# A four-layer graph network on one core: where masks are made, when they are counted, and how resident and loaded blocks are mixed

## The chip, the core and the metric

The kernel runs on one core of a Trainium2 chip. The metric is the device time of one execution in microseconds (us). The kernel before was run three times: 551.85, 552.71 and 555.07 us, median 552.71 us.

The engines are named as the profile names them: PE (matrix multiply, with PEld for its weight loads), DVE (vector), ACT (scalar), POOL (GpSimd) and SP, which here only issues transfers (DMAs). [...] A "q" after an engine's name in a profile line means its sequencer, which waits or issues and does not compute.

## The reference, cut to what matters

The input is a node matrix `x` (3327 x 64) and a dense weighted adjacency matrix `adj` (3327 x 3327). Four layers follow, each of the form `x = layernorm(x + layer(x, adj))`. The change touches the third and the fourth:

```python
# layer 2: two hops
for k in range(2):
    agg = adj @ x
    x = tanh(concatenate([agg, x], axis=1) @ W[k])
...
# layer 3: of each row's neighbours only the last 100 count, with weights halved step by step
support = input @ weight
mask = (adj != 0)
rank = cumsum(mask, axis=1)
deg = rank[:, -1:]
k = minimum(deg, 100)
pos = rank - (deg - k)
w = mask * where(pos > 0, 0.5 ** (k - pos), 0.0)
out = w @ support + bias
```

So layer 3 needs, for every entry of `adj`, whether it is nonzero (the mask), and how many nonzeros stand behind it in its row (a running count).

## The kernel before, in words

**Tiling.** The nodes are padded to 3328 and cut into 26 blocks of 128. The host hands over `adj` transposed, so one block of it is a 128 x 3328 tile of f32 (1664 KB): 128 neighbours on the partitions, all nodes along the free axis. A half of a block is 128 x 1664, and a chunk is 416 columns; there are four chunks in a half.

**Hop 1 and hop 2 of layer 2** (the loop `for k in range(2)`) go through the 26 blocks. For each block, `add` (the matmuls of L514) issues 8 pairs of matmuls of 416 columns, which add the block's share to the four accumulators. Seven blocks lie in SBUF for the whole layer (`kept`: 25, 24, 23, 22 and 20, 21, 19). The others come by DMA into four rotating buffers (`at_l`) and a fifth (`bt_l`), issued on SP (`block`, L216). Such a buffer is free again when the PE has added the block and the DVE has made its mask, so these two set when the next load is issued. Hop 2 takes 23 blocks in its loop (steps 0 to 22: five that hop 1 left in the buffers, then 0, 25, 1, 24, 2, 23, 3, 22, then 4 to 13), and blocks 20, 21 and 19 after it, in `chunk_end`.

**Masks and counts beside hop 2.** Layer 3 needs, before it starts, for each block and each node how many nonzeros stand in the blocks behind it. For that, each block gets a bf16 mask on the DVE and 8 small matmuls on the PE (`t_counts`, L451), which add the block's column counts to two accumulators `t`. There are two kinds of mask:

- scratch masks (`t_masks`, L444), used for the count alone. They are made half by half into the tile `tm`, which holds one block; hop 2 has seven of them (blocks 0 to 6). A new one must wait until the PE has counted the last one.
- resident masks (`both_masks`, L353), which stay for layer 3. They are written over f32 blocks that hop 2 has already added: one f32 block has room for two bf16 masks (`slots_of`). The table `place` says at which step which mask goes where. Nine are made: block 25 into the tile `over` at step 1, blocks 24 and 23 at step 6, 22 and 20 at step 8, 21 and 19 at step 12, and the last two of the loop at steps 21 and 22.

When all 26 blocks are counted, `t_out` (L461) moves `t` to SBUF as `tb`, POOL writes it to DRAM as `t_rows` (L463), and `rows_of` (L431) reads one row of it back into the first partition of each resident mask.

**Between hop 2 and the loop of layer 3** ("the prologue" below) the last three blocks are added chunk by chunk (`chunk_end`), ACT takes tanh, the DVE adds the layer's input (`with_x2`, L725), and the layer norm and the node products of layer 3 follow in four groups of blocks A, B, C, E: `finish` (PE), `squares` (ACT), `sums`, `roots`, `factor`, `x3_of`, `rest_of` (DVE).

**The loop of layer 3** has 52 steps, 26 for each half. Step q: `count` (L644) multiplies mask q with a triangular matrix into one of two PSUM banks c = 0, 1; `read` turns the count into a weight by taking the bits of an integer (ACT at L659, or DVE at L657); `products` (L861) multiplies the weight with `support`, three steps later. Every seventh step the PE also does the low part of the products (L878). A count of the next step must wait until its bank is read. Bank 0 is always read by ACT, bank 1 by the DVE in odd steps and by ACT in even ones.

The masks of blocks that are not resident are loaded again by halves (`load`, L345, 832 KB each, four buffers `ah`), made on the DVE (`masks`, L366, six buffers), and get their first row from `t_rows` by a small DMA (L368). There are 34 of them, one at most in a step. SP issues in each such step the row and then the next load. The list `steps` puts seven of the nine resident blocks first in half 0, and spreads the other two among the 17 loaded ones.

A list `with_step` gives one small piece of remaining work to each of the first steps. At the fourth, `firsts_weighted` runs three DVE instructions (L478 to L480), which make the weights of the first rows from `tb` and a tile `m0`; `m0` holds one of the six mask buffers until then. At the seventh, `first_rows` (L893, L897) issues 16 small DMAs on POOL into `sf`, which the products four steps before the end of a half need (`first_products`, L904).

Order of the DVE's instructions in a step of the loop before, which the prediction uses:

```python
read(1, q, q % 2 == 1)          # DVE in odd steps
with_step.pop(0)()              # the step's piece of other work
masks(to_mask.pop(0))           # if a mask buffer is free
```

Of the kernel before, what the change touches and what calls it, by code (L numbers as in the profile page):

```python
# [81 lines left out]
def kernel(  # L82
# [230 lines left out]
    def layers(ctx, x2, x3, begun_here, kept, ready, ahead_ctx, strm):  # L313
# [168 lines left out]
        with tc.tile_pool(  # L482
# [6 lines left out]
            for k in range(2):  # L489
# [37 lines left out]
                if k:  # L527
                    end = [jb for jb in kept if jb not in soon]
                    r = len(order)
                    for jb in soon:  # L530
                        order += [others.pop(0), jb]
                    order += others
                    place = {
                        1: [(soon[0], over)],
                        r + 1: list(zip(soon[1:3], slots_of(soon[0]))),
                        r + 3: list(zip((soon[3], end[0]), slots_of(soon[1]))),
                        r + 7: list(zip(end[1:], slots_of(soon[3]))),
                    }
                    for i, at in zip((-2, -1), slots_of(soon[2])):
                        place[len(order) + i] = [(order[i], at)]  # L540
# [45 lines left out]
                for i, jb in enumerate(order):  # L586
# [6 lines left out]
                    if i or not k:  # L593
                        for c in range(CPH):
                            add(c, jb)
                    if k and len(t_made) > 2 * BATCH_T:
                        t_counts()
                    if jb not in t_done and jb not in kept and (k or i >= FIRST_T):
                        t_masks(jb)
                        if len(t_made) >= len(t_at):  # L600
                            t_counts()
                    if k:
                        for b, at in place.get(i, ()):
                            both_masks(b, at)
                    if k == 0 and begun_here:

                        if i == 8:
# [2 lines left out]

                            warm_t = small.tile([P, 1], F32, tag="warm", name="warm_t")
                            nc.scalar.activation(warm_t, hT[:, :1], AF.Tanh)
                    if k and len(t_done) == NB and not t_ends:
                        t_ends.append(i)
                        t_counts()
                        t_out()
                        rows_of(resident)
                if k:
# [266 lines left out]

        def first_rows():

            with nc.allow_non_contiguous_dma(reason="one row of each block"):
                for cg in range(CPH):
                    e = cg % 2  # L890
                    for h in range(2):
                        at = slice(cg * 32 + h * NBH, cg * 32 + (h + 1) * NBH)
# [129 lines left out]
        first_out = None  # L1022
        with_step = [
            lambda: other_parts(B), lambda: first_part(C), lambda: rest_of(C),
            lambda: (other_parts(C), firsts_weighted()), lambda: first_part(E), lambda: rest_of(E),
            lambda: (other_parts(E), first_rows()), lambda: x3_later(C), lambda: x3_later(E),
        ]
        products(0, 0)
        advance(1, 2)
        products(0, 1)  # L1030
        for q in range(LEAD, len(steps) + LEAD + 1):
            turn = q == NB + LEAD
            read(0, q, False)
# [5 lines left out]
            while consumed and consumed[0] <= q:  # L1039
                consumed.pop(0)  # L1040
# [1006 lines left out]
```

## Time and profile before

| what | value |
|---|---|
| median of three runs | 552.71 us |
| the profiled execution | 552.03 us |
| its span (first to last instruction) | 550.2 us |
| busy: PE, DVE, ACT, POOL | 93%, 71%, 53%, 42% of the span |
| hop 2, from its second step to its last (327.98 to 404.46 us) | 76.48 us, PE busy 71.86 |
| prologue (404.46 to 425.01 us) | 20.55 us, PE busy 18.24 |
| loop of layer 3, first stretch (425.01 to 479 us) | 53.99 us, PE busy 47.36 |
| loop, change of halves (479 to 500 us) | 21.00 us, PE busy 18.20 |
| loop, rest (500 to 537 us) | 37.00 us, PE busy 36.51 |

The span begins at the first instruction and ends at the last; the execution's own time is 1.8 us more. Times of day below are counted from the span's start. The stages were told apart by the lines of their instructions: hop 2 is where L514 reads `at_l`, `bt_l` and `kept` for the second time, the prologue begins with the first `chunk_end` that follows, and the loop with the first L861.

How to read the lines: in the timeline each line has the start, the length, the engine, the source line, the operation, what it writes and reads, the form, and how many instructions were merged; in brackets, how long the engine sat idle before it, and what released it. In the view of waits, each line names who waited, for whom, how long in total, how often, and the longest wait.

### The profile page before, as it was taken

The numbers are of one execution on the slowest core, as the hardware profiler recorded it, in microseconds if no ns is written. First come the engines' busy times: TensorE is split into PE (matmuls) and PEld (weight loads), VectorE is DVE, ScalarE is ACT, GpSimd is POOL, SyncE is SP. The second block draws the span as 40 slices with busy tenths as digits, with TensorE's granted clock in tenths as the row PEclk, the third lists the DMA queues.
The fourth block names the chain that finished last, engine by engine and source line by source line (L and its number), as shares of the span: only waits on it lengthen the run. The fifth ranks groups of instructions, "written<-read, shape, count | busy, mean of one in ns | idle before, by whom it ended". The sixth has DMA issues, their size and how long they took to land. (4 is left out here: it accounts for less than half of the span.)

```text
span 550.2 us, 7634 instructions
## 1 busy us (share of the span) xinstructions
PE 509.8 (93%) x2865; PEld 210.8 (38%) x2865; DVE 390.7 (71%) x563; ACT 293.3 (53%) x345; POOL 232.6 (42%) x121
## 2 busy tenths in 40 slices
PE   8889999999999999999999999888998789989992
PEld 5522222222222222854433354333444344454542
DVE  6899999999999999799444231637137986666314
ACT  4899999999999997610000000000016755566641
POOL 4599999999999998000000000000260280000000
PEclk9999999999999999899999999989999999999996
DMA  8978766666766545799998019957963799975001
GB/s 287 366 227 293 244 222 224 240 215 220 238 215 233 184 147 226 299 418 427 424 424 368 0 31 408 412 186 269 414 209 102 259 372 395 404 291 188 0 1 37
DMA packets 34137, 139.20 MB, mean 253 GB/s; under 512 B 11199, under 2 KB 12977, under 8 KB 28971
## 3 DMA queue, kind: packets, MB, share of 16 engines
q1 hardware_dynamic: 30571, 137.40, 67.3%
q0 software_dynamic: 1184, 0.63, 0.5%
q10 hardware_dynamic: 2336, 0.59, 0.5%
q8 instruction: 24, 0.39, 0.3%
q14 instruction: 22, 0.18, 0.1%
HBM read 136.93 MB, written 1.04 MB: 251 GB/s over the span
## 5 line engine op out<-in xcount | busy, mean ns | idle before, releaser
L1260 POOL TENSOR_TENSOR sg<-sg,at 128x1664 f32<-128x1664 f32 x44 | 163.6, 3738 | 1.3 <-ACT sg L1248 1.2
L1288 ACT ACTIVATE pq<-pq,al,ga 128x832 f32<-128x832 f32 x104 | 104.7, 1011 | 10.8 <-DVE a L1287 10.5
L1275 PE MATMUL pq<-riT,ljT 64*128 64x416 f32 x416 | 100.8, 561 | 10.4 <-DVE v L1296 6.2
L1296 DVE SCALAR_TENSOR_TENSOR v<-pq,a 128x832 f32<-128x832 f32 x104 | 105.8, 1018 | 3.2 <-ACT pq L1288 2.2
L1287 DVE SCALAR_TENSOR_TENSOR a<-pq,sg 128x832 f32<-128x832 f32 x104 | 105.7, 1016 | 0.5 <-PE prep_fours L1366 0.4
L1305 PE MATMUL acc<-v,xv 128*64 128x416 f32 x416 | 95.3, 537 | 0.0
L514 PE MATMUL cnt<-at_l,lj 128*64 128x416 f32 x496 | 90.1, 514 | 0.1
L1248 ACT ACTIVATE sg<-lb,rb 128x1664 f32<-128x1664 f32 (+1 forms) x53 | 87.2, 1649 | 0.0
L623 ACT ACTIVATE x<-cnt 128x416 f32<-128x416 f32 x8 | 4.1, 517 | 151.2 <-PE cnt L514 151.2
L659 ACT ACTIVATE w<-cnt 128x832 int16<-128x832 f32 x79 | 65.6, 864 | 34.9 <-PE cnt L644 34.4
L463 POOL DMA_DIRECT2D t_rows<-tb x4 | 2.6, 711 | 148.7 <-DVE tb L461 148.6
L1275 PEld LDWEIGHTS pq<-riT,ljT 64*128 64x128 f32 x416 | 31.3, 184 | 83.7 <-DVE v L1296 82.9
L514 PEld LDWEIGHTS cnt<-at_l,lj 128*64 128x64 f32 x496 | 34.9, 137 | 50.6 <-issue 49.3
L861 PE MATMUL acc<-w,s 128*128 128x416 bf16 x208 | 52.5, 339 | 1.3 <-DVE sq L765 0.5
L1305 PEld LDWEIGHTS acc<-v,xv 128*64 128x64 f32 x416 | 20.6, 134 | 61.8 <-issue 58.0
L657 DVE TENSOR_SCALAR w<-cnt 128x832 int16<-128x832 f32 x25 | 25.5, 1022 | 25.6 <-PE cnt L644 25.6
L514 PE MATMUL cnt<-kept,lj 128*64 128x416 f32 x224 | 43.4, 533 | 0.0
L366 DVE TENSOR_SCALAR mask<-ah 128x1664 bf16<-128x1664 f32 x34 | 35.5, 1058 | 7.0 <-DMA ah<-in_adjT 5.1
L644 PE MATMUL cnt<-mask,tri 128*128 128x416 bf16 x136 | 34.8, 338 | 6.0 <-DVE w L657 3.5
L444 DVE TENSOR_SCALAR tm<-at_l 128x1664 bf16<-128x1664 f32 x20 | 19.5, 1022 | 21.1 <-PE t L451 21.1
L644 PEld LDWEIGHTS <-tri 128*128 128x128 bf16 x208 | 19.5, 97 | 34.4 <-issue 17.7
L1260 POOL TENSOR_TENSOR sg<-sg,kept 128x1664 f32<-128x1664 f32 (+1 forms) x10 | 30.0, 3017 | 0.0
(316 smaller groups left out, 455.5 us busy)
## 6 DMA issues: line engine op xcount, KB each, us to landing
at_l<-in_adjT SPq DMA_DIRECT2D x27, 1664.0 KB, 11.7
at<-in_adjT SPq DMA_DIRECT2D x44, 832.0 KB, 4.8
ah<-in_adjT SPq DMA_DIRECT2D x34, 832.0 KB, 6.4
kept<-in_adjT SPq DMA_DIRECT2D x7, 1664.0 KB
bt_l<-in_adjT SPq DMA_DIRECT2D x6, 1664.0 KB
lb<-lf_rows SPq DMA_DIRECT2D x2, 384.0 KB, 5.7
mask<-t_rows SPq DMA_DIRECT2D x34, 3.2 KB
ljT<-ljT SPq DMA_DIRECT2D x4, 128.0 KB, 3.9
```

What stands on the lines that cost most here:

```text
L366: nc.vector.tensor_scalar(mask[q], ahead.pop(q), 0.0, None, ALU.not_equal)
L514: nc.tensor.matmul(acc[c][h * D : (h + 1) * D, :], hw[:, slot(jb), :], blocks[jb][:, o : o + CW], start=c not in begun, stop=last, skip_gr ...
L644: nc.tensor.matmul(cnt[c][:, e, :], tri, mask[q][:, of], start=True, stop=True, skip_group_check=True,)
L659: nc.scalar.activation(w.bitcast(I16), cnt[c], AF.Relu)
L861: nc.tensor.matmul(acc[h, c][:, e, :], s12[:, slot(jb)].rearrange("p t d -> p (t d)"), ws[q, c][:, e, :], start=first, stop=last,)
L1248: nc.scalar.activation(sg[:, :, of], lbs[:, :, of], AF.Sigmoid, bias=rb[:, sl : sl + 1])
L1260: nc.gpsimd.tensor_tensor(sg[:, :, of], sg[:, :, of], at[:, :, of], ALU.mult)
L1275: nc.tensor.matmul(pq[:, h, :], ljT[h != jb // NBH][rows, of], riT[rows, ch * CW : (ch + 1) * CW], start=True, stop=True,)
L1287: stt(a_s[t], pqs[t], CUBIC_PLUS, us.pop(t), op0=ALU.add, op1=ALU.mult)
L1288: nc.scalar.activation(pqs[t], pqs[t], AF.Square, bias=al[:, one], scale=ga[:, one])
L1296: stt(w, pqs.pop(t), CUBIC_REST, a_s.pop(t), op0=ALU.add, op1=ALU.mult)
L1305: nc.tensor.matmul(accs[cp, ci][h * D : (h + 1) * D, :], xv[:, slot(jb), :], w[:, h, :], start=(jb == orders[cp][0]), stop=(jb == orders[c ...
```

## The change

In hop 2:

- The table `place` has one resident mask in each of its steps instead of two: block 25 at step 1 as before, 24 at step 7, 22 at 9, 20 at 10, 21 at 13, 19 at 14, 23 at 17, and the last two as before.
- From step 6 on, scratch masks take turns between `tm` and the first half of block 25's space, which is free from then until block 23's mask goes there at step 17.
- `t_counts` is called in each step after the step's adds, and before the step's masks are made, so that a mask is counted in the step after the one in which it was made. The last one is counted at step 18, where it was step 15; `t_out` and the rows follow there.

Between hop 2 and the loop: three of the 34 `masks` are called in the prologue, one after `with_x2(2)`, two after `rest_of(B)` and before `sums(E)` on the DVE.

In the loop: in half 0, five resident blocks come first instead of seven, and four are spread among the loaded ones. Bank 1 is read by the DVE in odd steps and also in even steps in which no mask is made. `firsts_weighted` comes at the tenth step (q = 12) alone instead of the fourth (q = 6). The 16 small DMAs of `first_rows` are issued on SP instead of POOL, two in each of the eight steps after it (q = 13 to 20).

```diff
-                        1: [(soon[0], over)],
-                        r + 1: list(zip(soon[1:3], slots_of(soon[0]))),
-                        r + 3: list(zip((soon[3], end[0]), slots_of(soon[1]))),
-                        r + 7: list(zip(end[1:], slots_of(soon[3]))),
+                        1: (soon[0], over),
+                        r + 2: (soon[1], in_first[1]),
+                        r + 4: (soon[3], in_second[0]),
+                        r + 5: (end[0], in_second[1]),
+                        r + 8: (end[1], in_last[0]),
+                        r + 9: (end[2], in_last[1]),
+                        r + 12: (soon[2], in_first[0]),
...
-                    if k and len(t_made) > 2 * BATCH_T:
+                    if k:
                         t_counts()
+                    if k and i == r + 1:
+                        t_at = halves_of(in_first[0]) + t_at
                     if jb not in t_done and jb not in kept and (k or i >= FIRST_T):
                         t_masks(jb)
-                        if len(t_made) >= len(t_at):
+                        if k == 0 and len(t_made) == len(t_at):
                             t_counts()
-                    if k:
-                        for b, at in place.get(i, ()):
-                            both_masks(b, at)
+                    if k and i in place:
+                        both_masks(*place[i])
...
-                    if k and len(t_done) == NB and not t_ends:
+                    if k and len(t_done) == NB and not t_made and not t_ends:
                         t_ends.append(i)
-                        t_counts()
                         t_out()
                         rows_of(resident)
...
-            n = len(here) - (7 if h == 0 else 0)
+            n = len(here) - (5 if h == 0 else 0)
...
             with_x2(2)
+            masks(to_mask.pop(0))
             finish(l3t, A)
...
             advance(0, 0)
+            masks(to_mask.pop(0))
+            masks(to_mask.pop(0))
             sums(E)
...
-                        nc.gpsimd.dma_start(
-                            sf[at, 0, :],
-                            s12[:1, h::2].rearrange("p n t d -> p n (t d)"),
-                        )
-                        nc.gpsimd.dma_start(sf[at, 1, e * D : (e + 1) * D], s3[:1, h::2])
+                    yield lambda at=at, h=h, e=e: (
+                        nc.sync.dma_start(
+                            sf[at, 0, :], s12[:1, h::2].rearrange("p n t d -> p n (t d)")
+                        ),
+                        nc.sync.dma_start(sf[at, 1, e * D : (e + 1) * D], s3[:1, h::2]),
+                    )
...
-            lambda: (other_parts(C), firsts_weighted()), lambda: first_part(E), lambda: rest_of(E),
-            lambda: (other_parts(E), first_rows()), lambda: x3_later(C), lambda: x3_later(E),
+            lambda: other_parts(C), lambda: first_part(E), lambda: rest_of(E),
+            lambda: other_parts(E), lambda: x3_later(C), lambda: x3_later(E), firsts_weighted,
+            *first_rows(),
...
+            while consumed and consumed[0] <= q:
+                consumed.pop(0)
+            at_work = len(consumed) - len(to_mask) + (m0 is not None)
+            one_more = bool(to_mask) and at_work < MASKS
             read(0, q, False)
...
-            read(1, q, q % 2 == 1)
+            read(1, q, q % 2 == 1 or not one_more)
...
-            if to_mask and len(consumed) - len(to_mask) + (m0 is not None) < MASKS:
+            if one_more:
                 masks(to_mask.pop(0))
```

More of the change, by code (lines that the diff above doesn't have):

```diff
@@ L532, in layers @@
                     order += others
+                    in_first, in_second, in_last = (slots_of(soon[i]) for i in (0, 1, 3))
                     place = {
-                        1: [(soon[0], over)],
-                        r + 1: list(zip(soon[1:3], slots_of(soon[0]))),
-                        r + 3: list(zip((soon[3], end[0]), slots_of(soon[1]))),
-                        r + 7: list(zip(end[1:], slots_of(soon[3]))),
+                        1: (soon[0], over),
[5 more added lines that the diff above has]
+                        r + 12: (soon[2], in_first[0]),
                     }
                     for i, at in zip((-2, -1), slots_of(soon[2])):
-                        place[len(order) + i] = [(order[i], at)]
+                        place[len(order) + i] = (order[i], at)
                     t_at = halves_of(tm)
@@ L886, in first_rows @@
         def first_rows():
[L888 to L892, printed above, removed]
-                        nc.gpsimd.dma_start(
-                            sf[at, 0, :],
-                            s12[:1, h::2].rearrange("p n t d -> p n (t d)"),
-                        )
-                        nc.gpsimd.dma_start(sf[at, 1, e * D : (e + 1) * D], s3[:1, h::2])
+            for cg in range(CPH):
+                e = cg % 2
+                for h in range(2):
+                    at = slice(cg * 32 + h * NBH, cg * 32 + (h + 1) * NBH)
+                    yield lambda at=at, h=h, e=e: (
[4 more added lines that the diff above has]
+                    )
         def first_products(h):
@@ L1035, in layers @@
                 first_out = half_out(0, sums_out(0))
-            read(1, q, q % 2 == 1)
+            read(1, q, q % 2 == 1 or not one_more)
             if with_step:
                 with_step.pop(0)()
-            while consumed and consumed[0] <= q:
-                consumed.pop(0)
-            if to_mask and len(consumed) - len(to_mask) + (m0 is not None) < MASKS:
+            if one_more:
                 masks(to_mask.pop(0))
```

## The prediction

> **What bounds the kernel now.** I read the shares of busy time first, then the five stages of the table above, then, stage by stage, who waits for whom. The PE is 93% busy, so only its idle time, and the work that stands between hop 2 and the loop, can be won or lost. Hop 2 leaves it idle for 76.48 - 71.86 = 4.6 us, the prologue for 2.3, the loop up to 479 us for 6.6, the change of halves for 2.8, the rest for 0.5.
>
> The PE's timeline in hop 2 shows what it waits for:
>
> ```profile
> 342.10 0.54 PE L451 MATMUL t<-over,upto 128*32 128x416 bf16 x8
> 342.46 0.53 PE L451 MATMUL t<-tm,upto 128*32 128x416 bf16 x8
> 342.92 3.02 PE L514 MATMUL cnt<-kept,lj 128*64 128x416 f32 x16
> ...
> 348.65 0.54 PE L451 MATMUL t<-kept,upto 128*32 128x416 bf16 x8
> 349.71 0.54 PE L451 MATMUL t<-kept,upto 128*32 128x416 bf16 x8 [0.52 <-DVE kept L353]
> 350.65 0.36 PE L451 MATMUL t<-tm,upto 128*32 128x416 bf16 x4 [0.40 <-DVE tm L444]
> 351.58 0.36 PE L451 MATMUL t<-tm,upto 128*32 128x416 bf16 x4 [0.57 <-DVE tm L444]
> 351.87 3.01 PE L514 MATMUL cnt<-kept,lj 128*64 128x416 f32 x16
> ...
> 360.82 4.71 PE L514 MATMUL cnt<-kept,lj 128*64 128x416 f32 x16
> ```
>
> At 342.10 two blocks are counted in 0.82 us. At 348.65 three blocks take 3.22 us, because the DVE makes their masks just then. The last line is an add of 4.54 us (to 365.36) where others take about 2.84.
>
> The DVE's timeline beside it shows that it works at that time and stands still before, held by the PE:
>
> ```profile
> 345.96 3.70 DVE L353 TENSOR_SCALAR kept<-kept 128x3328 bf16<-128x3328 f32 x2 [9.39 <-PE cnt L514]
> 349.57 1.96 DVE L444 TENSOR_SCALAR tm<-at_l 128x1664 bf16<-128x1664 f32 x2
> ```
>
> In the loop the same two views, the PE's and then the DVE's timeline, at the place of the largest wait:
>
> ```profile
> 436.96 0.51 PE L644 MATMUL cnt<-mask,tri 128*128 128x416 bf16 x2 [2.34 <-DVE w L657]
> 448.53 0.53 PE L644 MATMUL cnt<-mask,tri 128*128 128x416 bf16 x2 [0.47 <-DMA mask<-t_rows]
> 450.79 0.53 PE L644 MATMUL cnt<-mask,tri 128*128 128x416 bf16 x2 [0.67 <-ACT w L659]
> ```
>
> ```profile
> 432.17 0.58 DVE L478 TENSOR_SCALAR m<-m 128x832 f32<-128x832 f32 x1
> 432.79 1.02 DVE L479 SCALAR_TENSOR_TENSOR m<-tb,m 128x832 f32<-128x832 bf16 x1
> 433.85 1.19 DVE L480 TENSOR_SCALAR tb<-m 128x832 int16<-128x832 f32 x1
> 434.96 1.01 DVE L366 TENSOR_SCALAR mask<-ah 128x1664 bf16<-128x1664 f32 x1
> 435.89 1.01 DVE L657 TENSOR_SCALAR w<-cnt 128x832 int16<-128x832 f32 x1
> ```
>
> The read at 435.89 stands behind 3.7 us of other DVE work, and the PE waits 2.34 us for it.
>
> **What the Trainium skill says.** "TensorE: Matmul & The Clock Gate", section "What's actually happening": the array's clock is halved after a window of little activity and freed again after a busy one. The trace agrees: the granted clock is 0.83 between 360 and 370 us and 1.00 around it, and pairs of matmuls start 0.68 us apart from 360.9 to 364.3, against 0.35. It comes after two of the waits. "DMA: Bandwidth & Descriptors", section "Issuing engines are not separate DMA queues": transfers from SP and POOL share the same 16 engines, so moving the small `sf` transfers to SP saves only issue time on POOL, which bounds nothing here (42% busy, and idle from 453 us on). No run yet shows such transfers on SP.
>
> **The change part by part. Hop 2.** Before, the 14 block counts (blocks 25, 0, 24, 23, 1, and so on) take 0.82 + 3 x 3.22 + 3 x 0.47 = 11.9 us. After, each is counted a step after its mask: six alone and four in pairs, 6 x 0.47 + 4 x 0.82 = 6.1 us, if the masks are ready. I checked this by laying the steps end to end from 328.0 us, 2.8 us an add. Three examples: block 1's mask needs block 25's add (345.2), so it and block 24's are made from 345.3 to 349.2 and counted at 351.5; block 22's mask needs block 24's add (351.4) and is ready at 353.3 for a count at 358; block 5's and 19's are ready at 370.5 for 375. None is late. Saved: 5.8 us. More counting groups cost about 0.1 us each at their edges (adds next to counts last 2.84 to 2.89, others 2.8): +0.3. With the waits gone I expect the slow clock gone: -1.75 (bounds 0 and -1.75). The last load's wait of 0.3 us goes: -0.3. Sum: **-7.6 us**, from 404.5 to 396.9.
>
> What is late next would be the loads. A buffer is free once added and masked, so loads are issued sooner: the load of block 9, issued at 377.39 before, leaves with block 4's add, now at about 368.5. From that issue to the landing of the last load (401.6) the trace has 24.2 us, at a DMA share near 1; that gives 392.7, and the PE wants it at 394. So the margin is about 1.2 us; a shortfall of 1 to 2 us here belongs to the range. `t_out` stays where it was (384.4), although three steps later. The rows of the resident masks were read from 397.65 on; the first is needed 9.4 us after hop 2, at 406 now, and landed 4.1 us after its issue.
>
> **Prologue.** The three masks cost the DVE 0.94 us each (1.02 less the overlap that the pitch of two shows). The first stands before `sums(A)`, which began 0.86 us after `with_x2(2)`: +0.1 if its load has landed. It was issued at 404.67, and `with_x2(2)` ends at 410.0; loads take 5.4 to 7.4 us. Landing after 5.4 us costs +0.2, after 6.4 +1.2, after 7.4 +2.2, and everything on the DVE up to `finish(E)` is queued behind it. With four loads alone in the queues I take +0.6. The other two fill an idle time of 1.32 us before `sums(E)` with 1.88 of work: +0.5. Prologue: **+1.1 us** (0.6 to 2.7).
>
> **Loop.** Four terms.
> - The 2.34 us wait at step 6 goes, as `firsts_weighted` leaves it: -2.3.
> - The waits for late masks and their rows (0.47 at 448.53, 0.67 at 450.79, 1.17 at 466.64) should shrink, since three masks are made ahead and four resident blocks stretch the time between loads. I take half: -1.2 (0 to -2.3).
> - `firsts_weighted` comes back at step 12. Between the DVE's reads of steps 11 and 13 stand: a read 0.95, `x3_later` 0.6, a mask 0.94, the three instructions 2.87, a mask 0.94, in all 6.3 us, where two steps take about 3.1. The PE has no stock of counts to fall back on, as a bank must be read before the next count: +3.2 (2.5 to 3.5).
> - The extra DVE reads. A DVE read is 1.02 us against ACT's 0.86; in the undisturbed steps after 503 us, a step whose bank 1 the DVE reads takes 1.60 us, the other 1.56. For a dozen such steps that is +0.5. Just after the change of halves, a read comes between the two DVE instructions that scale the output (0.68 and 0.48 us, L967) and delays the next: +0.7. Sum +1.2 (0 to 2.5).
>
> The spread itself adds no work: it only reorders the same 52 steps. The `sf` transfers add 16 issues of about 0.3 us on SP, which has waits of 1.3 to 3 us in each step to hide them. Loop: **+0.9 us**.
>
> Total: -7.6 + 1.1 + 0.9 = -5.6 us on the profiled 552.03, so 546.4. The median of the runs shown lies 0.68 above the profiled execution: **547 us**.
>
> **The rivals.**
> - *More is won.* The loads keep ahead of the loop (all 2.3 us of late masks go), the first mask finds its load landed (+0.6 for the prologue), the extra reads cost nothing: 552.7 - 7.6 + 0.6 - 2.3 - 2.3 + 3.2 = 544.3, less another 1 us of small waits for ACT in the first steps: **543**. For it speaks that ACT is relieved of reads; against it, that the early waits of 0.25 to 0.3 us are for ACT's bank 0, which doesn't change.
> - *The gain is given back.* The slow clock stays (-5.8 in hop 2), the first mask waits for its load (+2.7), step 12 costs 3.5, the extra reads 2.5 and late masks stay: -5.8 + 2.7 - 2.3 + 3.5 + 2.5 = +0.6, less the hop's 0.3 for the last load: **553**. In its favour: each bound is seen in a row. Against it: all must fall together.
> - *Slower: SP's queue.* In the program's order SP's transfers carry completion counts that go round over eight, and an issue waits for the one eight before. Two issues a step reach back four steps; with the `sf` transfers, steps 13 to 20 have four and reach back two. If a load still takes 6.4 us with only two in flight, a step gets its load every 3.2 us instead of 2.05: 8 x 1.15 = 9.2 us, on top of 547: **556**. Against it: with two in flight a load should wait less for others, and up to six masks are in stock. It decides only if the stock is down to about one at step 13.
>
> **How the numbers follow.** A measurement of this kernel can't tell less than about 0.5% (2.8 us) from no change. Forecast (544 to 549.5): 0.62. More is won: 0.18. The gain is given back: 0.12. Slower: 0.08. The range takes in most of the second case and the better part of the third, 542 to 551, and leaves out about 0.18. Faster by over 0.5% (under 549.9): 0.62 + 0.18 + 0.02 = 0.82; within 0.5%: 0.10; slower 0.08.
>
> **What would show it right or wrong.** Right: hop 2's last add ends near 397 us, no wait of the PE for `tm` or `kept` in it, and no clock of 0.83 there; the largest PE wait of the first half moves to about step 13 and is about 3 us, behind L478 to L480; `sums(A)` begins 6.5 to 7.5 us after hop 2's end. Wrong: PE waits for `at_l` at the end of hop 2 (the loads became the bound), waits for `mask<-t_rows` while SP issues `sf`, or a DVE idle of over 2 us before the first mask in the prologue.

## The result, and the profile after

| | before | after |
|---|---|---|
| median of 20 runs each, run side by side | 554.27 us | 548.20 us |
| range of these runs | 551.71 to 557.65 | 544.91 to 555.40 |
| ratio, with its 95% interval | | 0.9889 (0.9865 to 0.9913) |
| the profiled execution / its span | 552.03 / 550.2 us | 547.23 / 545.4 us |
| hop 2, second step to last | 76.48 us | 69.08 us |
| prologue | 20.55 us | 21.02 us |
| loop of layer 3 to the last instruction | 125.24 us | 127.06 us |

The ratios leave out the few executions that took over 1.5% longer than the fastest of the same kernel; the medians and ranges take in all.

The kernel is 6.1 us faster by the medians and 4.8 us by the two profiled executions, of which the one before lies 2.2 us under its median and the one after 1.0. In those, hop 2 gives 7.40 us, the prologue takes back 0.47 and the loop 1.82; hop 2 also began 0.30 us later, which is the work ahead of it varying (328.0 to 330.9 us over all kernels below).

Stages of the profile after, from its table of windows (length; busy time and number of instructions of PE, PEld, DVE, ACT and POOL; granted clock, DMA share, GB/s): hop 2, prologue, loop up to the products of step 10, from there to step 26, and the rest but the very end.

```profile
328.28:397.36 69.08, 69.08 (x465) 26.52 (x466) 31.63 (x26) 0.00 (x0) 6.70 (x10) 1.00 0.87 349
397.36:418.38 21.02, 18.25 (x91) 9.19 (x88) 15.20 (x46) 10.26 (x18) 6.62 (x12) 1.00 0.78 264
418.38:438.61 20.23, 18.65 (x111) 9.34 (x111) 17.48 (x20) 14.56 (x21) 3.66 (x3) 1.00 0.88 321
438.61:480.70 42.09, 37.98 (x244) 20.32 (x243) 29.06 (x31) 21.31 (x26) 0.00 (x0) 0.96 0.88 316
480.70:543.60 62.90, 50.03 (x328) 26.28 (x327) 34.38 (x52) 25.13 (x33) 0.00 (x0) 0.96 0.27 83
```

In the first line the PE is busy for the whole of hop 2, at full clock: its 4.6 us of idle time are gone, and 2.8 us of busy time too (71.86 before). The fourth line, which holds the loop's largest wait, leaves the PE idle for 4.1 us at a clock below 1. Of the 12.9 idle us of the last line 8.2 lie after 532.5 us, where the loop's products have ended.

The PE's timeline of the profile after in hop 2, at the place where three blocks took 3.22 us before, and below it a line of the DVE's:

```profile
345.81 0.54 PE L451 MATMUL t<-tm,upto 128*32 128x416 bf16 x8
346.28 3.01 PE L514 MATMUL cnt<-at_l,lj 128*64 128x416 f32 x16
349.12 2.96 PE L514 MATMUL cnt<-kept,lj 128*64 128x416 f32 x16
352.01 0.89 PE L451 MATMUL t<-kept,upto 128*32 128x416 bf16 x16
352.83 3.01 PE L514 MATMUL cnt<-at_l,lj 128*64 128x416 f32 x16
```

```profile
346.85 1.89 DVE L353 TENSOR_SCALAR kept<-kept 128x3328 bf16<-128x3328 f32 x1
```

One block is counted in 0.47 us, two in 0.82, and no bracket appears. The DVE's line is the last mask of the two blocks counted at 352.01: it was ready at 348.74, 3.3 us before its count.

The PE's timeline after in the loop, at the largest wait, and the DVE's beside it:

```profile
439.36 0.51 PE L868 MATMUL acc<-w,s 128*128 128x416 bf16 x2
442.34 0.51 PE L648 MATMUL cnt<-mask,tri 128*128 128x416 bf16 x2 [2.46 <-DVE w L661]
...
443.04 0.80 PE L648 MATMUL cnt<-kept,tri 128*128 128x416 bf16 x2
443.63 0.90 PE L868 MATMUL acc<-w,s 128*128 128x416 bf16 x2
444.32 0.90 PE L648 MATMUL cnt<-kept,tri 128*128 128x416 bf16 x2
```

```profile
437.21 1.02 DVE L366 TENSOR_SCALAR mask<-ah 128x1664 bf16<-128x1664 f32 x1
438.14 0.58 DVE L478 TENSOR_SCALAR m<-m 128x832 f32<-128x832 f32 x1
438.76 1.03 DVE L479 SCALAR_TENSOR_TENSOR m<-tb,m 128x832 f32<-128x832 bf16 x1
439.82 0.59 DVE L480 TENSOR_SCALAR tb<-m 128x832 int16<-128x832 f32 x1
440.33 1.02 DVE L366 TENSOR_SCALAR mask<-ah 128x1664 bf16<-128x1664 f32 x1
441.27 1.02 DVE L661 TENSOR_SCALAR w<-cnt 128x832 int16<-128x832 f32 x1
```

The wait of step 6 has become a wait of step 12. The DVE works through its instructions in the order of the program and without a gap, so the read at 441.27 stands behind 4.1 us of other work. After it pairs of matmuls start 0.69 us apart instead of 0.35, until 446.4.

SP's timeline after, in the steps that issue `sf` (start, length of the issue):

```profile
444.09 0.35 SPq L368 DMA_DIRECT2D mask<-t_rows  x1
444.49 0.35 SPq L345 DMA_DIRECT2D ah<-in_adjT  x1
444.89 0.81 SPq L900 DMA_DIRECT2D sf<-s  x1
445.75 0.75 SPq L903 DMA_DIRECT2D sf<-s  x1
...
448.11 0.35 SPq L345 DMA_DIRECT2D ah<-in_adjT  x1
```

Issuing a tiny `sf` transfer takes SP over twice as long as issuing an 832 KB load. From 441.67 to 465.49 SP issues nine loads, one every 2.98 us, where one came every 2.06 us before (17 from 447.58 to 480.52). SP now also waits with the issue of a load until an earlier load has landed. Its view of waits from 418 to 482 us has this line, and the profile before has none like it:

```profile
SPq L345 <- DMA ah<-in_adjT: 4.2, 5, 1.4
```

The PE's waits in the loop after, from the view of waits (total, how often, the longest):

```profile
PE cnt L648 <- DVE w L661: 5.4, 7, 2.5
PE cnt L648 <- ACT w L663: 2.9, 7, 1.4
```

Before, the same two were 3.9 us in 3 waits and 3.6 us in 8: three waits for the DVE's reads became seven.

### The profile page after: what moved, and what is told of

Same layout as the page of the kernel before. It is cut to its first block, busy times and chain, and to the rows that moved or that the text cites. A ratio compares the mean times of both kernels' runs of the same rounds, so it can differ in the third digit from the quotient of the medians.

```text
span 545.4 us, 7628 instructions
## 1 busy us (share of the span) xinstructions
PE 508.9 (93%) x2865; PEld 210.4 (39%) x2865; DVE 399.4 (73%) x573; ACT 285.3 (52%) x335; POOL 220.0 (40%) x105
## 4 chain that ended last, share of the span: by engine, by line
PE 64%; DVE 16%; ACT 10%; DMA 4%; issue 4%; DVEq 0%; SPq 0%; ACTq 0%
PE cnt L514 27%; PE pq L1285 12%; PE acc L1315 8%; DVE v L1306 5%; ACT pq L1298 4%; DMA ah<-in_adjT 4%; ACT sg L1258 4%; PE cnt L648 3%; DVE w L661 3%; PE acc L885 3%; PE acc L868 2%; PE t L451 2%; DVE mask L366 2%; DVE a L1297 1%; PE cnt L505 1%
## 5 line engine op out<-in xcount | busy, mean ns | idle before, releaser
L663 ACT ACTIVATE w<-cnt 128x832 int16<-128x832 f32 x69 | 57.8, 864 | 44.9 <-PE cnt L648 44.4
L463 POOL DMA_DIRECT2D t_rows<-tb x4 | 3.8, 1014 | 150.0 <-DVE tb L461 150.0
L661 DVE TENSOR_SCALAR w<-cnt 128x832 int16<-128x832 f32 x35 | 35.8, 1022 | 21.4 <-PE cnt L648 21.3
L514 PE MATMUL cnt<-kept,lj 128*64 128x416 f32 x224 | 41.6, 514 | 0.0
L444 DVE TENSOR_SCALAR tm<-at_l 128x1664 bf16<-128x1664 f32 x16 | 15.7, 1023 | 21.5 <-PE t L451 21.5
```

What stands on the lines that cost most here:

```text
L514: nc.tensor.matmul(acc[c][h * D : (h + 1) * D, :], hw[:, slot(jb), :], blocks[jb][:, o : o + CW], start=c not in begun, stop=last, skip_gr ...
L661: nc.vector.tensor_scalar(w.bitcast(I16), cnt[c], 0.0, None, ALU.max)
L663: nc.scalar.activation(w.bitcast(I16), cnt[c], AF.Relu)
```

## The experiments

The theory after the result: hop 2 is the whole gain, and the edits of prologue and loop give some 2 us of it back. Rivals: the later edits share in the gain; in hop 2 it is the places, not the later count; in the loop it is SP's transfers, or the extra reads, and not step 12. All times in this table are of the profiled executions, but for the median (of 6 runs; 20 for the kernels before and after, 7 for `weights_split`, 22 for `h2_counts_only`) and the ratio to the kernel before, run side by side. That kernel was run again with each group of kernels (medians 554.15 to 554.92 us), so kernels of different groups are best compared by their ratios. "0 to 10" is from the first products of layer 3 to those of step 10, and so on.

| kernel | hop 2 | prologue | 0 to 10 | 10 to 26 | 26 to end | median | ratio (95%) |
|---|---|---|---|---|---|---|---|
| before | 76.48 | 20.55 | 22.54 | 39.46 | 63.24 | 554.27 | 1 |
| after | 69.08 | 21.02 | 20.23 | 42.09 | 64.74 | 548.20 | 0.9889 (0.9865 to 0.9913) |
| h2_all | 69.08 | 20.48 | 23.73 | 39.46 | 63.23 | 546.80 | 0.9871 (0.9840 to 0.9902) |
| h2_counts_only | 72.56 | 20.54 | 24.11 | 39.78 | 63.14 | 551.42 | 0.9950 (0.9932 to 0.9968) |
| h2_one_place | 70.25 | 20.69 | 23.80 | 39.82 | 64.59 | 549.79 | 0.9912 (0.9880 to 0.9944) |
| weights_split | 69.08 | 21.01 | 20.23 | 42.85 | 64.71 | 549.23 | 0.9907 (0.9873 to 0.9942) |
| split_sf_early | 69.08 | 21.01 | 20.44 | 45.64 | 64.71 | 546.81 | 0.9875 (0.9837 to 0.9912) |
| old_reads | 69.08 | 21.01 | 20.09 | 39.67 | 62.91 | 546.31 | 0.9865 (0.9825 to 0.9905) |
| sf_on_pool | 69.08 | 21.01 | 20.58 | 41.34 | 65.18 | 546.82 | 0.9874 (0.9847 to 0.9901) |
| split_old_reads | 69.08 | 21.02 | 20.09 | 44.28 | 63.11 | 546.33 | 0.9835 (0.9793 to 0.9877) |
| split_reads_pool | 69.08 | 21.01 | 20.53 | 39.31 | 63.27 | 544.76 | 0.9826 (0.9800 to 0.9853) |
| h2_split | 69.08 | 20.49 | 21.36 | 40.47 | 63.22 | 546.20 | 0.9839 (0.9808 to 0.9871) |
| no_early | 69.08 | 20.48 | 27.26 | 42.22 | 65.12 | 560.96 | 1.0121 (1.0089 to 1.0153) |
| seven_first | 69.08 | 21.01 | 19.91 | 47.45 | 65.34 | 549.31 | 0.9907 (0.9874 to 0.9940) |

Hop 2 is the same to 0.01 us wherever its code is the same; the loop's columns vary by about 1.5 us between executions, as its clock does (below). One profiled execution can lie well off the median of its kernel: `split_sf_early` was profiled at 551.28 us (median 546.81), `seven_first` at 555.49 (549.31), `sf_on_pool` at 549.42 (546.82), `old_reads` at 543.09 (546.31), `no_early` at 555.52 (560.96).

### Hop 2: the part alone, and its own parts

`h2_all` is the kernel before with the hop-2 edits alone. `h2_one_place` takes the second scratch place out of it:

```diff
-                    if k and i == r + 1:
-                        t_at = halves_of(in_first[0]) + t_at
```

`h2_counts_only` also has the old table `place`, with two resident masks in a step, so that only the later count is left:

```diff
-                    if k and len(t_made) > 2 * BATCH_T:
+                    if k:
                         t_counts()
...
```

> The kernel before with all of the change's hop 2 (places and later counts), and with the old prologue and loop. Theory 'hop 2 is the whole gain': hop 2 7.4 us shorter as in the changed kernel, prologue and loop as before, so 7.0 to 7.5 us faster than before (0.987), and about 1 to 1.5 us faster than the changed kernel. Rival 'the later edits share in the gain': 3 to 5 us faster than before (0.991 to 0.995), slower than the changed kernel, because the old loop meets its loads and masks just as late.

> The kernel before with the change's hop 2, but one scratch place (the tile tm) instead of two. Theory 'the later count is the gain': a scratch mask waits for the count of the one before, which now comes right after the adds of its step, so at most 0.5 us more than with two places: 6.5 to 7.4 us faster than before. Rival 'the second place is what lets counts wait': masks of blocks 3 to 6 start late and the counts after them wait some 0.5 to 1 us each: 3 to 5 us faster.

> The kernel before with one edit: counts are made in the step after the masks; the masks keep their old places, two resident ones in one step, one scratch tile. Theory 'the later count is the gain': the DVE needs 3.9 us in the steps with two resident masks but nobody waits for it in the same step, so 5.5 to 7.4 us faster than before (0.987 to 0.990). Rival 'the masks must also be spread': the counts of the steps with two resident masks and a scratch mask still wait for the DVE, about 1 us at each of three steps, and the slow clock stays: 2 to 4 us faster.

`h2_all`: 7.7 us faster by the medians and 7.40 in hop 2. So hop 2 carries the whole gain; the later edits add nothing to it that can be seen in the changed kernel (548.20, and the intervals overlap). The first theory stands for the whole part.

Inside it, both rivals had the size (4.7 us by the medians with one place, 3.0 with the counts alone), and neither theory had the reason. In the profiles the later count alone gives 3.92 us of the 7.40, spreading the resident masks 2.31 more, the second place the last 1.17; each was measured on top of the one before, and no other order was tried. But the missing part is not a wait for the DVE. All waits of `h2_counts_only` in hop 2 on the PE, in its timeline:

```profile
394.34 3.01 PE L514 MATMUL cnt<-at_l,lj 128*64 128x416 f32 x16 [1.18 <-DMA at_l<-in_adjT]
398.33 3.01 PE L514 MATMUL cnt<-at_l,lj 128*64 128x416 f32 x16 [0.98 <-DMA at_l<-in_adjT]
```

With the count a step later no count waits for a mask. The PE now waits for the last two loads: 2.29 of the 3.48 us that this kernel lacks in hop 2 are idle time (the PE is busy for 70.27 us, 1.19 more than in `h2_all` with the same matmuls, which was not pursued). The DVE's timeline of the same kernel shows why they are late:

```profile
361.07 1.96 DVE L444 TENSOR_SCALAR tm<-at_l 128x1664 bf16<-128x1664 f32 x2 [2.01 <-PE t L451]
366.96 3.69 DVE L353 TENSOR_SCALAR kept<-kept 128x3328 bf16<-128x3328 f32 x2 [3.93 <-PE cnt L514]
370.57 1.95 DVE L444 TENSOR_SCALAR tm<-at_l 128x1664 bf16<-128x1664 f32 x2
```

A scratch mask stands behind 3.69 us of resident masks or waits until `tm` is counted; until it is made, the load buffer that it reads isn't free. The load after the mask of 370.57 was issued at 372.59, 44.0 us after the start of hop 2; in the changed kernel the same load goes out 41.0 us after it. In `h2_one_place` the view of waits names the same two, in hop 2:

```profile
DVE tm L444 <- PE t L451: 20.4, 5, 9.3
PE cnt L514 <- DMA at_l<-in_adjT: 0.8, 1, 0.8
```

The DVE's 20.4 us of waits for `tm` cost nothing by themselves; the load that they delay costs the PE 0.83 us at the end. Counted from the start of hop 2, the mask of the last loaded block starts at 65.16 us after the change, 67.39 with one place and 69.70 with the counts alone. So the spread and the second place pay chiefly as earlier loads.

### Step 12: the weights of the first rows

`weights_split` runs the three instructions of `first_weights` in steps 12, 13 and 14 of the changed kernel; with that, the transfers of `sf` come two steps later:

```diff
...
-            lambda: other_parts(E), lambda: x3_later(C), lambda: x3_later(E), firsts_weighted,
+            lambda: other_parts(E), lambda: x3_later(C), lambda: x3_later(E),
+            firsts_weighted, firsts_weighted, firsts_weighted,
             *first_rows(),
```

> The changed kernel with the three instructions of the first rows' weights in three steps (q = 12, 13, 14) instead of one. Theory 'one step's DVE queue is the loss': the PE wait of 2.46 us at step 12 and the slow clock after it (about 1.6 us) go, small waits of 0.2 to 0.5 us come back: 2 to 4 us faster than the changed kernel, 8 to 10 us faster than before (0.982 to 0.986). Rival 'the DVE is short of time over all these steps': the same 2.5 us of work delays three reads by 0.6 to 1 us each, the PE waits as much in sum and only the slow clock may go: 0 to 1.5 us faster than the changed kernel.

No gain: 549.23 us. The rival had the waits right: spread over three steps the same work still costs the PE 0.78 us at 441.05 and 1.15 at 445.29, in all 1.93 where it was 2.46. By step 20 the loop was 3.0 us ahead of the changed kernel; about half of that is the slow clock, which did not come (1.46 us, below). It lost them just after, in a wait that my edit had made and in a slow clock that followed (0.68 in the 5 us after the wait):

```profile
466.03 0.35 PE L915 MATMUL acc<-tb,sf 32*128 32x416 bf16 x3
468.63 0.97 PE L915 MATMUL acc<-tb,sf 32*128 32x416 bf16 x5 [2.25 <-DMA sf<-s]
469.54 0.87 PE L872 MATMUL acc<-w,s 128*128 128x416 bf16 x2
```

The products of step 22 need all of `sf`, whose last transfer now came two steps later. So the next kernel issues `sf` from step 12 on, beside the three instructions:

```diff
...
+            for k, issue in enumerate(rows):
+                yield lambda k=k, issue=issue: (firsts_weighted() if k < 3 else None, issue())
...
```

> As weights_split, but the transfers of sf begin at step 12 again (12 to 19, beside the three instructions). In weights_split the loop won 3.0 us up to product 20 and lost them in a 2.25 us wait for sf, issued two steps later, and a slow clock after it. Theory 'one step's DVE queue is the loss, and sf must not come later': both go, the wait for sf stays out, so 2 to 4 us faster than the changed kernel (0.982 to 0.985 of before). Rival 'the transfers land late in any case, as SP is behind with its issues': a wait of the PE for sf of 1 us or more is left at step 25, and the kernel is within 1.5 us of the changed one.

By the median it is 1.4 us under the changed kernel, with overlapping intervals. Four of its six executions took 545.17 to 547.35 us and two 551.28 and 551.48; the profile is of one of these two, and how the other four ran is not on record. In the profiled one the wait for `sf` is gone, and again nothing is won in products 10 to 26: 45.64 us. The rival was half right: SP is behind, but it is the loads that land late, not `sf`. The timelines of SP and, below it, of the DVE in this kernel:

```profile
445.76 0.35 SPq L345 DMA_DIRECT2D ah<-in_adjT  x1
...
452.20 0.35 SPq L345 DMA_DIRECT2D ah<-in_adjT  x1
...
458.64 0.35 SPq L345 DMA_DIRECT2D ah<-in_adjT  x1
...
465.15 0.35 SPq L345 DMA_DIRECT2D ah<-in_adjT  x1
```

```profile
445.84 1.03 DVE L366 TENSOR_SCALAR mask<-ah 128x1664 bf16<-128x1664 f32 x1 [0.40 <-DMA ah<-in_adjT]
...
452.28 1.03 DVE L366 TENSOR_SCALAR mask<-ah 128x1664 bf16<-128x1664 f32 x1 [1.05 <-DMA ah<-in_adjT]
...
458.72 1.03 DVE L366 TENSOR_SCALAR mask<-ah 128x1664 bf16<-128x1664 f32 x1 [2.47 <-DMA ah<-in_adjT]
...
465.25 1.03 DVE L366 TENSOR_SCALAR mask<-ah 128x1664 bf16<-128x1664 f32 x1 [2.01 <-DMA ah<-in_adjT]
```

SP issues each of these loads 0.08 to 0.10 us before the DVE starts on another load that has just landed. That other load is the one issued two loads, or eight issues of SP, before: the load of 445.76 takes 6.4 us to land, and the next line of SP is at 452.20. The view of waits names the landing as what SP waits for:

```profile
SPq L345 <- DMA ah<-in_adjT: 6.4, 6, 1.5
```

It isn't the buffer: the one that the load of 452.20 fills was last read by the mask of 445.84. From 418 to 482 us this wait occurs in each of the seven kernels that issue `sf` on SP (1.4 to 6.7 us in all) and in none of the seven that issue it on POOL (`before`, the four kernels `h2_`, `sf_on_pool`, `split_reads_pool`). Two loads every 6.5 us are 3.2 us each, the very figure of the rival "SP's queue". The DVE waits for `ah` 14.5 us in all from 418 to 482 us (6.2 after the change), its reads stand behind those masks, and the PE waits for them up to 2.9 us. With less lost at step 12, the PE reached steps whose loads were not there yet.

### The extra reads, and sf on POOL

`old_reads` takes the new rule for bank 1 back, and `sf_on_pool` issues the transfers of `sf` on POOL, in the same place of the program:

```diff
-            read(1, q, q % 2 == 1 or not one_more)
+            read(1, q, q % 2 == 1)
```

```diff
-                        nc.sync.dma_start(
+                        nc.gpsimd.dma_start(
...
-                        nc.sync.dma_start(sf[at, 1, e * D : (e + 1) * D], s3[:1, h::2]),
+                        nc.gpsimd.dma_start(sf[at, 1, e * D : (e + 1) * D], s3[:1, h::2]),
```

> The changed kernel with the old rule for bank 1 (DVE in odd steps alone). Theory 'the extra reads cost': from product 26 to the end the kernels with the old rule take 1.8 us less (10.49 and 37.5 us against 11.44 and 38.4 for products 26 to 31 and 31 to 51), so 1.5 to 2.5 us faster than the changed kernel. Rival 'the extra reads relieve ACT in the first 26 products': the gain after product 26 is given back before it by waits for ACT of 0.3 to 0.7 us in five or more steps: within 0.5 us of the changed kernel.

> The changed kernel with the 16 transfers of sf issued on POOL, in the same steps 13 to 20. Theory 'SP's issues delay the loads but not the PE': the loads come earlier, the DVE waits less for ah from 450 to 470 us (4 us in sum there now), and the loop changes by less than 0.7 us. Rival 'SP is the bound of these steps': products 13 to 26 (33.5 us) take 1 to 3 us less. A third, 'POOL gets in the DVE's way': masks beside POOL's work take 1.7 us instead of 1.0, and the loop is 1 to 3 us longer.

`old_reads`: 1.9 us less than the changed kernel by the medians, within what was expected, though the two intervals overlap. The profile, of the fastest of six executions, places it: 1.83 us after the products of step 26, and 1.18 from products 13 to 26 (32.33 against 33.51). The waits of its PE in the loop:

```profile
PE cnt L648 <- DVE w L661: 2.9, 2, 2.5
PE cnt L648 <- ACT w L663: 2.9, 7, 1.4
```

Five of the seven waits for DVE reads are gone, and not one for ACT has come: ACT needed no relief.

`sf_on_pool`: 546.82, 1.4 us less, again with overlapping intervals. POOL isn't held up by the steps' masks, as SP is, and issued `sf` from 434.2 to 446.7 us (442.1 to 464.6 on SP). From products 13 to 26 it took 32.6 us (33.5), and the DVE's waits for `ah` up to 482 us fell from 6.2 to 1.9 us. In these steps the PE gains slightly more than the first theory allowed (0.9 against 0.7); the whole loop took 127.10 us in this execution and 127.06 in the changed kernel's. The third theory, POOL in the DVE's way, shows nothing: the masks from 432 to 446 us took 1.02 us.

Before product 26 the two aren't separate losses. The changed kernel's PE waits for the DVE's reads at 456.64 and 458.70, 1.05 us in all. Both are gone with the old reads, and with `sf` on POOL, where the extra reads stay, one of 0.30 is left. It took an extra read and a late load together.

### Put together

> split_sf_early with the old rule for bank 1, the version put together from what seemed to cost: if both terms add up, 4 to 5.5 us faster than the changed kernel (543 to 544 us where the changed one has 548.2, 0.978 to 0.981 of before). Rival 'the edits hide one another' (with the old reads ACT becomes late in the first steps): no better than the better one of the two alone, 545 to 546 us.

> split_old_reads with the transfers of sf issued on POOL instead of SP (steps 12 to 19). In split_sf_early SP issued a load at 445.76, 452.20, 458.64 and 465.15 us, each 0.01 to 0.02 us after the load issued two loads before it had landed. Theory 'SP's completion counts are the bound once step 12 is cured': on POOL the loads come faster, the waits of 0.8 to 2.9 us for the DVE's reads between products 16 and 26 go, and the loop takes 120 to 122.5 us (127.06 in the changed kernel, 127.5 and 130.8 in the two split ones): 541 to 543.5 us, 0.976 to 0.981 of before. Rival 'the loads are bound by what the DMA engines can move': the waits stay behind ah on POOL too, 545 to 547 us.

> The kernel before with the change's hop 2 and one more edit: the three instructions of the first rows' weights in steps 6, 7 and 8 instead of all in step 6; everything else of the loop, sf on POOL among it, as before. Theory 'that queue on the DVE and the slow clock after it are the loop's largest loss': products 0 to 10 take 20.0 to 21.0 us (23.73 in h2_all, 20.23 in the changed kernel), so 2 to 3.5 us faster than h2_all: 543 to 545 us. Rival 'the first steps have no slack on the DVE (11.9 of 12.6 us busy)': the wait is only spread, 0 to 1 us faster than h2_all.

`split_old_reads` is `split_sf_early` with the old reads: 546.33 by the median, 0.9835 by the ratio, which can't be told from the old reads alone (546.31, 0.9865). In the profiled execution products 10 to 26 take 44.28 us, with the DVE waiting 11.5 us for `ah`. With `sf` moved to POOL, and nothing else changed, they take 39.31 us, and the kernel 544.76: its interval lies wholly below that of the changed kernel, but not below that of `split_old_reads`. What differs between these two is the spread: six executions from 542.06 to 551.05 us with `sf` on SP, and from 544.47 to 545.68 on POOL. So the queue of SP is shown as the loss of the profiled execution, and a gain in the middle of many executions is not shown. I had expected up to 543.5, and 544.76 lies above it; the loop's 123.1 us miss the 122.5 expected by little. The longest wait of its PE for a read of the DVE is 0.87 us.

This version has the lowest median and ratio of those run: hop 2 and prologue of the change, old reads, weights in three steps, `sf` on POOL. By the ratios `h2_split` (0.9839) can't be told from it, and is the simplest: hop 2 alone, and the three instructions in steps 6, 7 and 8 of the old loop. It took 546.20, 0.6 us less than `h2_all` by the medians and 1.8 by the ratios, with overlapping intervals, where 2 to 3.5 were expected; in the profiles products 0 to 10 fell by 2.4 us, but 10 to 26 took 1.0 more. Its PE waited 2.1 us for rows of masks in the loop (0.3 in `h2_all`); `m0` holds a mask buffer two steps longer there, which was not tried apart.

### The prologue masks and the order of the blocks

`no_early` takes the three `masks` out of the prologue; `seven_first` puts seven resident blocks first again:

```diff
-            n = len(here) - (5 if h == 0 else 0)
+            n = len(here) - (7 if h == 0 else 0)
```

> The changed kernel without the three masks in the prologue. Theory 'they are the stock that covers SP's slow loads in steps 13 to 20': the prologue is 0.5 us shorter (20.5), but the PE waits for the DVE's reads, which stand behind masks that wait for ah, 2 to 6 us in sum between products 13 and 26: 2 to 5 us slower than the changed kernel. Rival 'a mask is made in each step anyway, so the stock is made up by step 12': waits as in the changed kernel, 0 to 0.7 us faster than it.

> The changed kernel with the old mix: seven resident blocks first in half 0, two among the loaded ones. Theory 'the spread stretches the loads': with two instead of four resident steps among the 17 loaded ones the loads are wanted faster, SP can't follow in steps 13 to 20, and the PE waits 1 to 4 us more: 1 to 4 us slower than the changed kernel. Rival 'the order is neutral': the seven steps without a load build the same stock at the start, within 0.7 us of the changed kernel.

`no_early` is slower than the kernel before: 560.96. The sign was as the theory said, the size and the place were not: 7.0 us are lost before the products of step 10, where no `sf` is issued yet. Its PE's timeline:

```profile
424.76 0.51 PE L648 MATMUL cnt<-mask,tri 128*128 128x416 bf16 x2 [1.88 <-DMA mask<-t_rows]
428.39 0.51 PE L648 MATMUL cnt<-mask,tri 128*128 128x416 bf16 x2 [2.06 <-DMA mask<-t_rows]
```

With five resident blocks first, the first loaded mask is wanted two steps sooner than with seven; made in the loop, it and its row come too late. `h2_all`, with seven first and no mask in the prologue, has one such wait in its loop, of 0.28 us. So five resident blocks first need the three masks in the prologue here. The profiled execution was the fastest of its six (555.5; the others took 559.6 to 562.9), so some 5 us of the median are not in its profile, and where they go wasn't tried.

`seven_first` is 1.1 us slower than the changed kernel by the medians, with overlapping intervals. Its profiled execution was the slowest of six (555.5): products 10 to 26 took 47.45 us, the DVE waited 13.3 us for `ah`, and SP issued each second load just as the one eight issues before landed, as in `split_sf_early`.

## Why the prediction was right, and where its steps failed

The time was right: 547.0 forecast, 548.2 measured, a change of -5.6 forecast, -4.8 in the profiled pair and -6.1 in the medians. The likeliest case came about. That the total fits so well is in part luck: the prologue was put too high by 0.6 us and the loop too low by 0.9, and inside the loop terms missed by 0.7 to 1.4 us in both directions. The base moved too: over 20 runs the kernel before has a median of 554.27 us, where the three known ones gave 552.71.

- **Hop 2, -7.6: right**, -7.40. The counts shrank as worked out, and the slow clock went. The margin of the last load, given as 1.2 us, was about 1.1: the mask of the last block, which waited for that load, started at 393.44, and its add, the last third of the 8.38 us from 388.98 to 397.36, began at about 394.57. But the sum treats spread and second place as though they only let the counts be ready; the runs showed that 3.5 of the 7.4 us hang on them, mostly through the loads. `t_out` did not stay at 384.4; it came at 386.09, without cost.
- **Prologue, +1.1: too high**, +0.47. The mis-sized term is the first mask's wait for its load (+0.6). The mask began 402.83, directly after `with_x2(2)`, and took 1.17 us beside other work; `sums(A)` began 6.56 us after hop 2, against 6.41 before. The four loads were issued from 397.57 on, and there was no wait, so the first had landed within 5.3 us, at the fast end of the 5.4 to 7.4 us allowed for.
- **Loop, +0.9: too low**, +1.82. By terms: the wait of step 6 gone, -2.3 as forecast (products 0 to 10 took 2.31 us less). The late masks: 2.31 us of waits before (the 0.67 among them is by its line a wait for ACT, just after a late row), one of 0.20 left, so -2.1 and not half of it. Step 12: a wait of 2.46 instead of 3.2, but also a slow clock that the sum did not hold, worth 1.46 us (below), so 3.9 in all. Extra reads: +1.2 with bounds of 0 and 2.5; measured +1.50 after the products of step 26, and +1.05 in the two waits at 456.64 and 458.70, which took the late loads as well. With these it is 2.6, and 3.0 by `old_reads`, above the upper bound; this term was sized worst. I priced a DVE read against an ACT read in a quiet step, and not the masks that a read can stand behind.
- **`sf` on SP at nothing: the price was wrong**, 0.79 and 0.75 us an issue, not 0.3. With a row and a load that is 2.2 us of issues a step, more than a quiet step's 1.6. The Trainium skill, "DMA: Bandwidth & Descriptors", section "Issuing engines are not separate DMA queues", says that issuing on several engines saves only issue time, usually small beside the transfer. Here that time was not small for an engine that also issues the loads. In the changed kernel it cost 0.9 us between products 13 and 26, of the same waits that the extra reads share, and 1.4 us by the medians, where the intervals overlap.
- **The rival "slower: SP's queue"** did not come about, but its mechanism is real. SP's waits for a landing are there in the changed kernel (4.2 us), and the eight issues and the 3.2 us a load were measured in `split_sf_early`. That the stock of masks, its condition, kept the loss small is likely but not shown: `no_early`, which has three masks less, loses its 7.0 us before the first `sf` transfer.

## What to carry to other kernels

When a wait goes, ask at once what has been using its time: in the executions profiled here, spreading the work of step 12 won nothing over products 10 to 26 until the issues of small transfers had left the queue of the loads. A buffer's reader on another engine counts as much as the PE for when the buffer is free, so a mask made earlier can pay as a load issued earlier. Before moving work between engines, look whether the waits for the one to be relieved would go: those for ACT stayed at 2.9 us in 7 waits with and without the extra reads.

## What the runs showed of the hardware

- **Issue time does not follow the size of a transfer.** In the changed kernel's loop an 832 KB load took SP 0.33 to 0.35 us to issue, a row of 3.2 KB 0.24 to 0.37, and an `sf` transfer of 3.2 KB 0.79 to 0.94, one of 1.6 KB 0.75 to 0.82. An `sf` transfer spreads one partition over 13; what about it makes the issue long was not tried.
- **The slow clock after a wait comes in some executions only.** The Trainium skill, "TensorE: Matmul & The Clock Gate", section "What's actually happening", says that the clock is halved after an idle window of about 3.4 us. Halved fits: pairs of matmuls started 0.69 us apart instead of 0.35. The length does not: no wait in these loops was that long. Of the 13 PE waits of over 2 us (2.06 to 2.86) in the loops of the fourteen profiles, nine had a mean clock of 0.66 to 0.73 in the 5 us after them and four had 1.00; some of the waits of about 1.4 us were followed by it too. From products 10 to 13, with the same wait of 2.46 to 2.50 us, the windows of the changed kernel and of `old_reads` are:

```profile
438.61:447.19 8.58, 6.12 (x26) 2.87 (x25) 7.33 (x9) 3.15 (x5) 0.00 (x0) 0.80 0.88 296
```

```profile
438.69:446.03 7.34, 4.66 (x25) 2.32 (x24) 7.00 (x9) 3.40 (x5) 0.00 (x0) 1.00 0.88 283
```

The PE was busy 1.46 us longer with the same work at a clock of 0.80. `sf_on_pool` had it (0.80), `seven_first` not (1.00) in the same step. After the wait of 2.34 us in step 6, `h2_all` had it and the kernel before had not, and 0 to 10 took 1.2 us more. So a wait of 2.3 to 2.5 us cost 1.2 to 1.5 us more than its length, in part of the executions.
